# Four engines issue in the order of the source, and the source emits the steps of all parts by a plan of engine times

## The chip, the cores and the metric

The kernel runs on one core of one Trainium2 chip. The metric is the device time of one execution in microseconds. The core has five engines that matter here: TensorE (PE: matrix products and transposes; PEld is its loading of weights), VectorE (DVE), ScalarE (ACT), GpSimd (POOL, which here issues the transfers that scatter and gather rows by an index) and SyncE (SP, which issues all other transfers). Each engine executes its own list of instructions and waits on semaphores for the others.

## The reference

Two macaron layers on 2048 tokens (2 sequences of 1024) of 256 numbers, all in 32-bit floats:

```
x = x + 0.5 * L0_ffn(layernorm(x))      # 8 experts of width 176, top 2, and a shared expert of width 352
x = x + L0_attn(layernorm(x))           # RWKV: time mix, then channel mix
x = x + 0.5 * L0_ffn(layernorm(x))
x = x + 0.5 * L1_ffn(layernorm(x))      # 32 experts of width 96, top 6, and a shared expert of width 192
x = x + L1_attn(layernorm(x))           # linear attention with rotary embedding: one sum over each sequence
x = x + 0.5 * L1_ffn(layernorm(x))

# an ffn: scores -> the top K experts of each token and their weights ->
g = silu(x @ w_gate[e]) * (x @ w_up[e]);  routed = sum over the K experts of weight * (g @ w_down[e])
out = routed + (silu(x @ sw_gate) * (x @ sw_up)) @ sw_down
```

## The kernel before, in words

x stays in SBUF as 16 tiles of 128 tokens. Each of the four ffn parts (`sparse_moe`) sorts the tokens by expert through DRAM:

- **Routing** (`ready`, in halves of 8 tiles): `prep` normalizes four tiles (L108 to L114 on DVE, a square root on ACT), transposes them on PE (L122), copies the result on ACT (L299), multiplies by the router (L303), and finds the top experts on DVE (L140 to L180). After two preps `plan` counts tokens by expert with two products (L336, L343) and computes a slot in DRAM for every pair of token and expert (to L392). After the second half `owners` finds which expert owns each block of 128 slots (`who`, L425 and L426).
- **Scatter** (L399): one transfer on POOL for each tile and each of its K experts writes the rows to their slots in `xs`. That is 16 transfers a half in L0 and 48 in L1.
- **Shared expert** (`shared`, L452 gates, L468 turn, L494 output, L501 the addition to x) and the pairs' weights (`weights`, DVE).
- **Blocks**: 39 blocks of 128 slots in L0, 127 in L1. A block is fetched (L509, SP), transposed (L518), copied (L522, ACT), multiplied with its expert's gate and up weights, whose number PE reads from `who` (L531), gated (L442 ACT, L443 DVE), turned (L468, L475), multiplied with the down weights (L546), copied (L554, DVE) and stored (L555, SP). The stages of five neighbouring blocks alternate. A fetch waits for all scatters.
- **Combine**: a transfer on POOL gathers the rows of one tile and one expert (L565) into one of eight buffers, and four calls later DVE adds them to x with their weight (L576). The first half's gathers wait for the blocks that can hold its rows (23 in L0, 79 in L1) and go beside the remaining blocks. The second half's wait for the last block.

Between the first and the second L0 ffn stands RWKV: eight jobs (time mix and channel mix on four groups of four tiles), `run` calling the preparation of the next job inside the one before it. Its weights are loaded by `load_rwkv` (L644 to L655), which also computes five small vectors 1 - v on DVE (L652). `fill_slots` writes zeros to all slots of `xs` ahead of time. The attention (`attend`, once for each sequence) normalizes and transposes eight tiles, then multiplies each with the input weights (L833), rotates, sums, transposes the queries (L883) and at last multiplies with a scaled output matrix (L908).

The order of instructions on each engine is chosen by the Tile framework's scheduler, which takes the source's order as priority and a cost model's times for when something can start. In the source the parts stand one after another. The first L0 ffn reads

```
m["dispatch"](0)      # ready and scatter of the first half
m["dispatch"](1)
load_rwkv(weights)
m["shared"](0)
...
finish(m["blocks"](2))
```

and a few pairs alternate by fixed rates: the first combine beside the last blocks (2 calls a block in L0, 1 in L1), the first L1 routing beside the last L0 blocks, the first attention beside the second combine of the first L1 ffn.

## Time and profile before

17 executions took 1743.61 to 1756.22 us, with a median of 1749.77. The profiled execution took 1746.8 us, and its span from the first to the last instruction is 1745.0 us, at a mean granted clock of 0.82.

| stage | us from the start | length |
|---|---|---|
| first L0 ffn: routing, scatter, shared | 0 to 130 | 130 |
| its blocks | 130 to 243 | 113 |
| its second combine | 243 to 269 | 26 |
| RWKV | 269 to 480 | 211 |
| second L0 ffn: routing, scatter, shared | 480 to 597 | 117 |
| its blocks | 597 to 722 | 125 |
| its second combine; first L1 ffn: routing, scatter, shared | 722 to 920 | 198 |
| its blocks | 920 to 1157 | 237 |
| first attention and second combine | 1157 to 1209 | 52 |
| second L1 ffn: routing, scatter, shared; second attention | 1209 to 1438 | 229 |
| its blocks | 1438 to 1675 | 237 |
| its second combine | 1675 to 1745 | 70 |

The stages are read from the first and last start of their lines (L518 and L554 for blocks, L692 for RWKV, L908 for the end of an attention). POOL was busy for 523.6 us, 497 of them with the 512 indirect transfers, 0.97 us each, of which two neighbours start 1.26 us apart.

### The profile page before, as it was taken

Reading aid. Unit: us, or ns where it says so; the run is one execution under the profiler, and the core shown is the slowest. Engines: PE = TensorE matmul, PEld = TensorE weight load, DVE = VectorE, ACT = ScalarE, POOL = GpSimd, SP = SyncE. Lnnn points to the kernel's source line nnn. Section 1 sums busy time; section 2 is a strip of 40 time slices with the busy share of each in tenths; the row PEclk is TensorE's granted clock in tenths of the full one; section 3 lists DMA queues with packets and bytes.
Section 4 is the critical chain, followed back from the end, with each engine's and each line's share of the span. In section 5 each row is a group of like instructions: output and inputs, shape, how many; then the busy total and the mean of one; then the engine's idle time right before and its main releaser. Section 6 shows DMA issues by size and latency. Waiting matters only on the chain.

```text
span 1745.0 us, 21541 instructions
## 1 busy us (share of the span) xinstructions
PE 1205.0 (69%) x5462; PEld 899.5 (52%) x5462; DVE 759.5 (44%) x2588; ACT 580.4 (33%) x1565; POOL 523.6 (30%) x559
## 2 busy tenths in 40 slices
PE   6599856899957997511549994795837409994830
PEld 5377533566745775411328983663514309873630
DVE  5322348666153234332414443657826604443433
ACT  4123225776341333300105541441402105541310
POOL 1500321111133003274630016225570550016246
PEclk8699987999977999855669996897768759996875
DMA  9503329200081133541215664542220125665543
GB/s 278 184 16 104 121 85 305 89 1 0 0 204 64 31 103 118 147 137 63 91 66 158 188 182 136 154 125 70 69 103 10 67 90 171 184 183 157 172 123 106
DMA packets 182911, 203.06 MB, mean 116 GB/s; under 512 B 40044, under 2 KB 165772, under 8 KB 182796
## 3 DMA queue, kind: packets, MB, share of 16 engines
q1 hardware_dynamic: 158220, 134.55, 25.9%
q0 software_dynamic: 24576, 67.14, 12.3%
q8 instruction: 52, 0.85, 0.2%
q14 instruction: 63, 0.52, 0.1%
HBM read 100.68 MB, written 100.93 MB: 116 GB/s over the span
## 4 chain that ended last, share of the span: by engine, by line
PE 42%; issue 24%; another core or an unknown queue 6%; DVE 5%; DMA 3%; POOL 3%; ACT 2%; POOLq 0%; SPq 0%; DVEq 0%; ACTq 0%
PE pg_L_b L531 12%; PE py_L_b L546 8%; PE px_L L518 4%; PE pkv_cm L704 3%; POOL yk_L L565 3%; PE pkk_cm L692 3%; PE pg_L L452 3%; DMA yk_L<-ys_L,idx_L 2%; PE ph_L_b L468 2%; PE py_L L494 2%; DVE x L576 1%; PE pk_tm L692 1%; PE pcr_cm L704 1%; DMA ys_L<-yb_L 1%
## 5 line engine op out<-in xcount | busy, mean ns | idle before, releaser
L565 POOL DMA_INDIRECT yk_L<-ys_L,idx_L x256 | 248.1, 969 | 733.3 <-DMA ys_L<-yb_L 481.1
L399 POOL DMA_INDIRECT xs_L<-xn_L,idx_L x256 | 248.9, 972 | 287.6 <-DVE who_L L426 77.8
L531 PE MATMUL pg_L_b<-L1gu,xbT_L 128*128 x1016 | 223.8, 346 | 12.8 <-issue 8.7
L443 DVE TENSOR_TENSOR h_L_b<-g_L_b,pg_L_b 128x96 f32<-128x96 f32 (+1 forms) x332 | 90.4, 273 | 325.2 <-ACT g_L_b L442 299.1
L522 ACT COPY xbT_L<-px_L 128x256 f32<-128x256 f32 x332 | 123.4, 373 | 243.6 <-PE px_L L518 208.8
L531 PEld LDWEIGHTS pg_L_b<-L1gu,xbT_L 128*128 128x128 f32 x1016 | 170.7, 202 | 18.5 <-issue 11.4
L576 DVE SCALAR_TENSOR_TENSOR x<-yk_L,wk_L,x 128x256 f32<-128x256 f32 x256 | 120.0, 480 | 124.1 <-DMA yk_L<-ys_L,idx_L 108.8
L546 PE MATMUL py_L_b<-L1down,hT_L_b 96*128 x508 | 162.3, 402 | 12.7 <-ACT g_L_b L442 4.5
L518 PE MATMUL px_L<-ident,xb_L 128*128 128x128 f32 x664 | 133.0, 283 | 52.1 <-issue 52.1
L554 DVE COPY yb_L<-py_L_b 128x256 f32<-128x256 f32 x332 | 140.6, 423 | 63.1 <-PE py_L_b L546 33.2
L468 PE MATMUL ph_L_b<-ident,h_L_b 128*96 128x128 f32 (+1 forms) x410 | 103.3, 283 | 66.7 <-issue 38.7
L442 ACT ACTIVATE g_L_b<-pg_L_b 128x96 f32<-128x96 f32 (+1 forms) x332 | 88.4, 266 | 181.3 <-PE pg_L_b L531 118.3
L518 PEld LDWEIGHTS px_L<-ident,xb_L 128*128 128x128 f32 x664 | 97.5, 148 | 90.0 <-issue 57.3
L531 PE MATMUL pg_L_b<-L0gu,xbT_L 128*128 x312 | 108.4, 470 | 1.1 <-issue 0.6
L475 ACT COPY hT_L_b<-ph_L_b 96x128 f32<-96x128 f32 (+1 forms) x332 | 93.1, 280 | 38.7 <-PE ph_L_b L468 19.0
L468 PEld LDWEIGHTS ph_L_b<-ident,h_L_b 128*96 128x96 f32 (+1 forms) x410 | 51.6, 128 | 97.3 <-issue 56.3
L546 PEld LDWEIGHTS py_L_b<-L1down,hT_L_b 96*128 96x128 f32 x508 | 81.2, 201 | 24.9 <-ACT hT_L_b L475 6.2
L452 PE MATMUL pg_L<-L0sgu,xTs_L 128*128 128x352 f32 x256 | 90.8, 493 | 0.0
L442 ACT ACTIVATE g_L<-pg_L 128x176 f32<-128x176 f32 (+1 forms) x96 | 29.8, 323 | 166.1 <-PE pg_L L452 93.5
L546 PE MATMUL py_L_b<-L0down,hT_L_b 88*128 x312 | 82.8, 388 | 1.1 <-ACT hT_L_b L475 1.1
L122 PE MATMUL pt_L<-ident,xn_L 128*128 128x128 f32 x128 | 25.9, 349 | 67.4 <-DVE mv_L L109 31.4
L501 DVE SCALAR_TENSOR_TENSOR x<-py_L,x 128x256 f32<-128x256 f32 x64 | 27.0, 422 | 97.2 <-PE py_L L494 47.0
(216 smaller groups left out, 1849.7 us busy)
## 6 DMA issues: line engine op xcount, KB each, us to landing
xb_L<-xs_L SPq DMA_DIRECT2D x332, 128.0 KB
ys_L<-yb_L SPq DMA_DIRECT2D x332, 128.0 KB
xs_L<-zero SPq DMA_DIRECT2D x1, 16256.0 KB
xs_L<-zero SPq DMA_DIRECT2D x1, 4992.0 KB
xs_L<-xn_L,idx_L POOLq DMA_INDIRECT x256
yk_L<-ys_L,idx_L POOLq DMA_INDIRECT x256
L1gu<-in_L_gate SPq DMA_DIRECT2D x8, 384.0 KB
L1gu<-in_L_up SPq DMA_DIRECT2D x8, 384.0 KB
```

The source lines that it names most:

```text
L399: d = nc.gpsimd.indirect_dma_start(out=xs, out_offset=bass.IndirectOffsetOnAxis(ap=idx[:, t, k : k + 1], axis=0), in_=xn[h][:, i, :], in_o ...
L442: nc.scalar.activation(g, pg[:, 0:width], AF.Silu)
L452: nc.tensor.matmul(pg, xT[half][:, c, i * P : (i + 1) * P], w["sgu"][:, c, u, :, :].rearrange("p z w -> p (z w)"), start=(c == 0), stop=(c ...
L468: nc.tensor.transpose(pt[0:m, k * P : (k + 1) * P], h[:, r : r + m], ident)
L475: nc.scalar.copy(hT[0:m, lo:hi, :].rearrange("p k t -> p (k t)"), pt[0:m, lo * P : hi * P])
L518: nc.tensor.transpose(px[:, c * P : (c + 1) * P], xb[:, c * P : (c + 1) * P], ident)
L522: nc.scalar.copy(xbT.rearrange("p c t -> p (c t)"), px[:, 0 : DC * P])
L531: nc.tensor.matmul(pg, xbT[:, c, :], w["gu"][:, c, bass.ds(e, 1), :, :].rearrange("p e z h -> p (e z h)"), start=(c == 0), stop=(c == DC - 1),
L546: nc.tensor.matmul(py, hT[0:HP, k, :], w["down"][:, bass.ds(e, 1), k, :].rearrange("p e d -> p (e d)"), start=(k == 0), stop=(k == C - 1),)
L554: nc.vector.tensor_copy(yb, py)
L565: d = nc.gpsimd.indirect_dma_start(out=yk, out_offset=None, in_=ys[0 : n * P, :], in_offset=bass.IndirectOffsetOnAxis(ap=idx[:, t, k : k + ...
L576: added = nc.vector.scalar_tensor_tensor(x[t], gathered.pop((t, k)), wk[:, t, k : k + 1], x[t], ALU.mult, ALU.add)
```

## The change

Two parts of the program, the first L0 ffn and everything from the second L0 ffn to the end, are put into `manual_schedule` for PE, DVE, ACT and SP: these engines issue in the order in which the source emits instructions. RWKV and POOL are left to the scheduler. Every part becomes a generator that yields, after each step, an engine and the time that the step takes on it. `side_by_side` keeps a clock for each part and for each engine, and always emits the next step of the part whose clock is earliest; `after` lets a part begin when named other parts have been emitted. The plan knows these times only; nothing of it is measured while the program runs.

```diff
+    free = dict.fromkeys(("PE", "DVE", "POOL"), 0.0)
+    def side_by_side(*parts):
...
+            n = min(able, key=lambda n: (clocks[n], n))
+            if clocks[n] > clock["now"]:
+                yield "until", clocks[n]
+            step = next(parts[n], None)
...
+                engine, us = step
+                clocks[n] = max(clock["now"], free.get(engine, 0.0)) + us
+                if engine:
+                    free[engine] = clocks[n]
...
             normalize(x[ts], xb, BT, sub)
+            yield "DVE", 3.4
+            yield "", 1.0
             for c in range(DC):
                 nc.scalar.copy(xT[h][:, c, o * P : o * P + TB], transposed(xb, c, sub))
+            yield "PE", 1.0
+            yield "", 1.0
...
             route(w, lg, sub, taken[:, ts, :], comb[:, ts, :])
+            yield "PE", 1.3
+            yield "DVE", 3.0 if K == 2 else 4.0
...
+                    yield "POOL", 1.28
...
                     nc.vector.scalar_tensor_tensor(x[t], py, 0.5, x[t], ALU.mult, ALU.add)
+                yield "PE", 0.0033 * (SH * DC + D)
...
-        def combine(h, lag=4):
+        def combine(h, lag=4, adding=True, late=None):
             pairs = [(t, k) for t in range(HT * h, HT * h + HT) for k in range(K)]
-            for n in range(len(pairs) + lag):
+            for n in range(len(pairs) + (lag if adding else 0)):
                 if n < len(pairs):
-                    gather(*pairs[n])
-                if n >= lag:
+                    gather(*pairs[n], back if n < 8 or late is None else late)
+                if adding and n >= lag:
                     add_back(*pairs[n - lag])
-                yield
+                yield "POOL" if n < len(pairs) else "", 1.3
+            done[f"combine{h}"] = True
...
-            side = combine(0)
-            for q in range(NBLK + 4):
-                if q < NBLK:
-                    fetch(q)
+            for q in range(-lead, NBLK + 4):
+                if 0 <= q + lead < NBLK:
+                    fetch(q + lead)
...
+                if q - 4 == first - 1:
+                    done["first"] = True
+                yield "PE", 0.00169 * DC * 2 * H + 0.00169 * C * D + 0.1 * (DC + C)
...
+        return [
+            after([(d, "ready0"), (d, "ready1")], m["scatter"](1)),
+            after([(d, "ready0"), *alone], shared_of(0), m["weights"](0)),
+            after(
+                [(d, "ready1"), (d, "shared0")],
+                shared_of(1),
+                m["weights"](1),
+                after([(d, "scatter0"), (d, "scatter1")], m["blocks"]()),
+            ),
+        ]
...
-            m["dispatch"](0)
-            m["dispatch"](1)
-            load_rwkv(weights)
-            m["shared"](0)
...
+            with tc.manual_schedule(engines=ORDERED):
+                load_rwkv(weights)
+                play(
+                    after([], m["ready"](0), m["ready"](1)),
+                    after([(d, "ready0")], m["scatter"](0)),
+                    *mixture(m),
+                    after([(d, "first")], m["combine"](0)),
+                )
+        for _ in m["combine"](1, adding=False, late=weights):
+            pass
...
+                for t in range(HT, NT):
+                    for k in range(w0["K"]):
+                        m["add_back"](t, k)
+                        tc.add_manual_dep(
+                            m["latest"]["add"], rw["latest"].name, NOSYNC, reason="rows come late"
+                        )
...
+    with tc.manual_schedule(engines=ORDERED):
+        play(
+            after([], m0["ready"](0), m0["ready"](1)),
+            after([(d0, "ready0")], m0["scatter"](0)),
+            after([(d0, "blocks")], then(last_weights)),
+            *mixture(m0),
+            after([(d0, "first")], m0["combine"](0)),
+            after([(d0, "combine0"), (d0, "blocks")], m0["combine"](1)),
+            after([(d0, "combine0")], m1["ready"](0)),
+            after([(d1, "ready0"), (d0, "combine1")], m1["scatter"](0)),
+            after([(d1, "ready0"), (d0, "combine1")], m1["ready"](1)),
+            *mixture(m1, [(d0, "blocks")]),
+            after([(d1, "first")], m1["combine"](0)),
+            after([(d1, "combine0"), (d1, "blocks")], m1["combine"](1)),
+            after([(d1, "combine0"), (d1, "blocks")], attend(0, moe_pool)),
+            after([(at, "done0")], m2["ready"](0)),
+            after([(d2, "ready0"), (d1, "combine1")], m2["scatter"](0)),
+            after([(d2, "ready0"), (d1, "combine1")], attend(1, moe_pool), m2["ready"](1)),
+            *mixture(m2),
+            after([(d2, "first")], m2["combine"](0)),
+            after([(d2, "combine0"), (d2, "blocks")], m2["combine"](1)),
+        )
```

Smaller edits go with it. The two preps of a half alternate. In the first L0 ffn the second half's 16 gathers are issued without their additions, eight of them into eight new buffers, and the additions are emitted after the first mixing of the first RWKV job. The fetch of a block is emitted two steps earlier. The attention's tile steps are shifted: the products of tile t stand before the sums and queries of tile t-1 (a step planned at 4.6 us of PE), and the two additions to x move into the sums. Scratch tiles of `weights` and `plan` move from the three "yb" buffers to the four "xb" buffers, and the tiles of an ffn are allocated when its half begins.

## The prediction

> **What bounds the kernel now.** I read the page first, then the table by stage, then the tensor engine's timeline inside the poorest stage, then the DMA queue's own timeline. The page says that no engine is full on average:
>
> ```profile
> span 1745.0 us, 21541 instructions
> ...
> PE 1205.0 (69%) x5462; PEld 899.5 (52%) x5462; DVE 759.5 (44%) x2588; ACT 580.4 (33%) x1565; POOL 523.6 (30%) x559
> ...
> PE   6599856899957997511549994795837409994830
> ...
> POOL 1500321111133003274630016225570550016246
> ...
> L565 POOL DMA_INDIRECT yk_L<-ys_L,idx_L x256 | 248.1, 969 | 733.3 <-DMA ys_L<-yb_L 481.1
> L399 POOL DMA_INDIRECT xs_L<-xn_L,idx_L x256 | 248.9, 972 | 287.6 <-DVE who_L L426 77.8
> ```
>
> The reader sees PE near full in the blocks and the RWKV part, and almost empty where POOL's digits are high: where rows are scattered (L399) and gathered (L565). The table by stage (columns: stretch, length, busy time of PE, weight loads, DVE, ACT, POOL, then granted clock, DMA share, GB/s) puts lengths to it:
>
> ```profile
> 0.00:36.00 36.00, 23.32 (x84) 17.52 (x85) 22.37 (x137) 15.05 (x24) 1.74 (x14) 0.88 0.95 283
> 36.00:130.00 94.00, 71.20 (x301) 53.89 (x300) 27.49 (x146) 23.56 (x67) 31.22 (x33) 0.81 0.38 113
> 504.00:597.00 93.00, 68.21 (x295) 51.32 (x294) 26.95 (x142) 23.05 (x67) 30.74 (x32) 0.83 0.23 70
> 722.00:920.00 198.00, 63.58 (x209) 43.35 (x207) 52.34 (x213) 17.24 (x41) 108.54 (x112) 0.59 0.34 106
> 920.00:1039.00 119.00, 118.60 (x750) 106.41 (x749) 55.59 (x165) 64.54 (x251) 0.00 (x0) 1.00 0.60 182
> 1039.00:1157.00 118.00, 82.25 (x401) 66.88 (x401) 58.72 (x180) 40.02 (x138) 46.11 (x48) 0.78 0.50 149
> 1249.00:1438.00 189.00, 81.77 (x305) 52.11 (x304) 78.34 (x296) 30.50 (x75) 94.29 (x96) 0.71 0.20 70
> 1560.00:1675.00 115.00, 78.57 (x391) 64.90 (x389) 49.47 (x138) 33.45 (x129) 46.29 (x48) 0.78 0.55 162
> 1675.00:1745.00 70.00, 0.00 (x0) 0.00 (x0) 23.24 (x48) 0.00 (x0) 45.35 (x48) 0.51 0.38 107
> ```
>
> The two L1 dispatch stages (198 and 189 us) hold 64 and 82 us of PE work. L1 blocks run at 1.42 us each until the gathers begin (the yb copies at 958.5 to 1015.3 are 40 blocks in 56.8 us) and at 4.1 us beside them (20 from 1038.0 to 1119.6). Inside the 198 us stage, PE's timeline shows why (start, length, work, idle before it):
>
> ```profile
> 781.48 1.11 PE L122 MATMUL pt_L<-ident,xn_L 128*128 128x128 f32 x4 [19.56 <-issue]
> 793.69 0.63 PE L303 MATMUL lg_L<-L1router,xTs_L 128*128 128x32 f32 x2 [11.09 <-issue]
> 804.89 3.19 PE L303 MATMUL lg_L<-L1router,xTs_L 128*128 128x32 f32 x14 [10.57 <-issue]
> 820.61 1.19 PE L336 MATMUL rank_L<-taken_L,before 128*128 128x256 f32 x2 [12.53 <-DVE taken_L L168]
> ```
>
> Nothing that these steps wait for is late; the fourteen products at 804.89 are read by ACT only at 818.31. PE itself crawls, and it does so beside requests that POOL issues back to back (one per 1.26 us from 751.1 to 810.5). I call this the crawl. It begins some 10 to 13 us after such a train begins: shared tiles start every 2.4 us from 841.0 to 845.8 in the train from 833, and the adds that follow come at 860.0, 871.3 and 882.5.
>
> **The change part by part.** No arithmetic operation is added or removed; order and buffers move. The working is against the profiled execution: 1745.0 us of span, 1746.8 us in all, 3 us under the median of 1749.8.
>
> *The five small DVE operations at the top (a loss).* The loads of the RWKV weights and the operations 1-mk and so on (L652) now stand first in the ordered part, ahead of the first normalization on DVE. Their loads stand behind the x, L0 and zero transfers on SP:
>
> ```profile
> 52.88 0.49 SPq L648 DMA_DIRECT2D v_cm_mk<-in_cm_mk  x1
> 53.41 0.47 SPq L648 DMA_DIRECT2D v_cm_mr<-in_cm_mr  x1
> ```
>
> SP's order up to here does not change. The issue is paced by earlier landings, and the scatters of 36 to 57, which shared the DMA engines, will not have begun; with 2.2 us to land (x: issued at 0.74, read at 2.93) I put the fifth operation at 53. The before kernel executed them at 76.0 to 80.3, where nobody waited. Everything on DVE queues behind them: the first normalization starts at 53 instead of 2.9, and PE, ACT and POOL wait for it. The first half's routing then takes the 22 us that it took with data at hand (480 to 502) instead of 33, and ends at 75 instead of 36.
>
> *Shared experts beside the second half's routing (L0, twice).* Before, only gates were pulled forward; the shared turns waited for the routing's last product (who_L, at 66 and 533). Now they alternate. PE work after the first routing: 16 tiles by 4.0 us (adds at 107.2, 111.2, 115.2) are 64, routing of the second half 8, the crawl beside two 20 us trains 5 (12 gates by 2.4 and 16 outputs by 1.7 are 56 us, 538 to 597 took 59), and 8 for PE reaching a routing step too early and for ACT's table loads (1.28 us each; ACT is busy 23.6 of 94 us, so most are covered). Sum 85. First dispatch: blocks at 75 + 85 = 160 against 130, **-30** (+9 if the loads did not gate it). Second: 503 + 85 = 588 against 597, **+8**. Ends for the pair: -45 and +22.
>
> *L0's second combine moved into RWKV's first job.* Blocks ended at 243 and the first RWKV product came at 269; the 16 adds stood between. They go behind the first mixing; 16 by 0.48 are 7.7 us of DVE, while the first jobs wait on DVE anyway (reciprocals of 3.3 us). Gathers use fresh buffers. **+5**; ends -8 and +13.
>
> *L1's first dispatch.* Let the L0 blocks end at 0 (722 before). Gathers 9 to 29, first scatter 29 to 90 (48 by 1.27). The shared half is 19 us of PE (8 by 2.4): from 8 to 20 at full pace, the rest in the crawl, at a quarter (14 us of routing products stood in 63 us, 755 to 818), to 48. The second routing, now behind it on PE, has 14 us of PE work: 8 to 10 in the crawl by 90, the rest and 12 of DVE chain to 105. Second scatter 105 to 166, blocks at 168 against 198: **+30**. Ends: 0 (the crawl deepens), and +45 (POOL alone: 29 + 61 + 61 + 2).
>
> The Trainium skill, "SBUF — State Buffer", section "Who interferes with whom", says that PE and ACT never wait on anyone and that DMA does not contend with a compute engine. By that rule the overlapped work runs at full pace and the three L1 terms here and below give 45 + 45 + 45 instead of 54 in all. The rows above contradict it, so the sum does not use it.
>
> *L1 blocks beside the first combine, twice.* 237 us now: 79 blocks by 1.42, 4 for the store, then the slow stretch. Calls come once per planned block as before, eight gather buffers allow POOL ten us of lead, and then each gather waits for an add. With PE at 0.4 pace while POOL issues (20 blocks, 28 us of work, in 71 us), a block lasts 1.42 + 0.6 by 1.25 = 2.17; 48 of them are 104: 112 + 4 + 104 + 5 = 225. **+12** each. Four calls are 5.2 us of lag; store, gather and landing take about 8 (gather at 1039.34, its add at 1042.60, 3.3 us, behind a store of 4 to 5), so DVE stalls once for 3 us, included. On SP, now in source order, a block's fetch stands three steps (4.3 us) ahead of its use with one store between; a fetch lands in 2.0 us (1429.19), so I cost that at nothing. Ends for each: -10 and +45.
>
> *Attention and last dispatch.* attend(0), 52 us, now in two shifted steps: **+3**. attend(1) shares PE with a shared half (19 us) that had been done during the routing (adds 1244.7 to 1259.2). From the routing's end at T: 64 us of PE work, 13 before the crawl, 14 in it to T+61, 37 behind: T+98 against T+93 (1249 to 1342). **-5**; ends -25 and +20. Scatter and last combine stay: the 70 us at the end have no PE to be put beside.
>
> Sum: -30 + 8 + 5 + 30 + 24 + 3 - 5 = +35, so 1746.8 - 35 = 1712 in a profiled run, 1715 against the median; I say 1713.
>
> **The rivals.**
> *The small operations do not gate the start.* Either DVE takes them late, or they land early. Then the first dispatch gains 9 instead of losing 30: 1674. For: x takes the same queue and lands by 15.5. Against: the v loads are issued behind 12 MB. Chance 0.14.
> *The adds pace POOL so that there is no train and no crawl beside the blocks.* The combine beside attend(0) (1160 to 1236, POOL held eleven times by an add) shows no crawl. Both block stages gain 47 instead of 12: 1713 - 70 = 1643. Chance 0.10.
> *The crawl eats it.* More PE work lies beside trains; the L1 dispatch and both block stages gain nothing: 1713 + 54 = 1767, slower. Chance 0.14.
> *The plan runs ahead of the engines.* Slower: PE reaches routing steps whose inputs are late and holds the tiles behind them. There are 16 preparations with three such places each (transposes, logits, rank), 48. The plan gives a normalization 4.4 us; the first one took 2.93 to 9.0, 6.1. At 1.7 us each that is 82: 1795. It decides from 35/48 = 0.7 us each. Against: the plan gives an L0 shared tile 3.17 us and it takes 4.0, so PE comes later than planned. Chance 0.20.
>
> **How the numbers follow.** Main 0.42, own range 1670 to 1745; rivals as above. Faster by over 0.2% (3.5 us, about what a measurement here can tell): 0.40 + 0.14 + 0.10 = 0.64. Slower: 0.34 less what falls within, 0.32. Same 0.04. The range 1640 to 1798 leaves out half of the 1643 case, half of the 1795 case and little else, under 0.2.
>
> **What would show it.** The first L108 on DVE near 53, with L652 before it; the first block (L518) at 160, and shared outputs (L494) before the second routing's end. From the last L0 block to the first L1 block 168 us. yb copies beside gathers 2.2 us apart. The last scatter behind attend(1) as now. A first L108 at 3 refutes the loss; copies 1.4 apart refute the crawl there; PE idle with a releaser on DVE or ACT before L122 and L303, 48 times, is the last rival.

## The result: 5.4% slower on the chip of the prediction, 3.2% slower on another kind of chip

The changed kernel took 1841.45 us (median of 8, 1838.32 to 1846.09) against 1748.37 us (median of 47): a ratio of 1.0535, 95% interval 1.0518 to 1.0552. Predicted were 1713 us and a gain. The profiled execution took 1851.15 us, 10 us above the median, and the lengths of stages below are its own. The page of the profile after, whose lines answer to those shown of before:

```profile
span 1849.1 us, 21526 instructions
...
PE 1257.9 (68%) x5462; PEld 921.5 (50%) x5462; DVE 801.2 (43%) x2588; ACT 558.1 (30%) x1551; POOL 521.0 (28%) x559
...
PE   0588986799978898633528997954635545998830
...
POOL 0231033111022103174360005455360071003546
...
L627 POOL DMA_INDIRECT yk_L<-ys_L,idx_L x256 | 247.1, 965 | 730.2 <-DMA ys_L<-yb_L 547.2
L455 POOL DMA_INDIRECT xs_L<-xn_L,idx_L x256 | 247.8, 968 | 379.9 <-DVE idx_L L446 128.1
```

The transfers cost POOL what they did, PE and DVE execute as many instructions as before (5462 and 2588), and PE's first digit has gone from 6 to 0. The two groups of low digits (3352, slices 18 to 21, and 54635545, slices 27 to 34) are the L1 dispatches, the second with both attentions, where PE was meant to become fuller. The table by stage after (columns as before: stretch, length, PE, weight loads, DVE, ACT, POOL, granted clock, DMA share, GB/s):

```profile
0.00:50.00 50.00, 0.00 (x0) 0.00 (x0) 0.53 (x3) 0.00 (x0) 2.06 (x15) 1.00 0.92 253
50.00:177.00 127.00, 93.19 (x384) 70.59 (x385) 54.07 (x272) 34.36 (x88) 31.03 (x32) 0.91 0.18 63
516.00:641.00 125.00, 96.89 (x388) 72.20 (x386) 52.04 (x260) 33.09 (x87) 31.58 (x33) 0.81 0.36 92
772.00:983.00 211.00, 79.78 (x220) 51.71 (x220) 60.40 (x228) 17.80 (x43) 108.43 (x112) 0.60 0.32 99
1114.00:1205.00 91.00, 76.52 (x398) 59.91 (x396) 48.33 (x139) 34.41 (x133) 45.74 (x48) 0.92 0.67 196
1205.00:1318.00 113.00, 62.78 (x194) 41.24 (x194) 85.44 (x286) 15.75 (x48) 47.37 (x48) 0.67 0.20 58
1318.00:1553.00 235.00, 109.57 (x340) 71.20 (x340) 90.81 (x310) 38.76 (x90) 92.73 (x96) 0.67 0.16 54
```

For 50 us POOL and DVE show 2.6 us of work and the others none. The first L1 dispatch, 198 before, lasts 211. The last one, 189 before, lasts 235; the first shared half has come into it (340 records of PE, before 305).

One more thing has to be known to read what follows. The kernel before took 1748 us on the chip of the prediction and 1760 on another, but 1589 to 1591 on five more that runs were given. (Each of these was met in one set of runs, so a lasting property of a chip is not told from its state at that time.) So each experiment is compared with the kernel before on its own chip, and I call the first kind *chips with the crawl*: it is the crawl, as the prediction named it, that the others lack. The same cuts on both kinds (us, from the starts of the same lines; "routed" is the first half's slots being known):

| stage | before, after: with the crawl | difference | before, after: without | difference |
|---|---|---|---|---|
| start to first L0 block | 130, 177 | -47 | 111, 158 | -47 |
| L0 blocks | 113, 111 | +2 | 113, 103 | +10 |
| RWKV, up to routed | 260, 253 | +7 | 260, 254 | +6 |
| up to first block of the second L0 ffn | 94, 100 | -6 | 74, 80 | -6 |
| its blocks | 123, 131 | -8 | 125, 117 | +8 |
| up to first L1 block | 199, 211 | -12 | 155, 151 | +4 |
| L1 blocks | 238, 222 | +16 | 230, 209 | +21 |
| first attention, second combine, up to routed | 92, 113 | -21 | 87, 105 | -18 |
| up to first block of the second L1 ffn | 189, 235 | -46 | 138, 174 | -36 |
| its blocks | 236, 225 | +11 | 226, 208 | +18 |
| rest | 71, 71 | 0 | 71, 71 | 0 |

There are three losses: the start (47 on either kind), the stretch around the two attentions (54 without the crawl), and what the crawl adds (before lost 155 us to it, after 219, so 64 more). The gains in the blocks are there, and larger where nothing crawls.

### The profile page after: what moved, and what is told of

It is laid out like the page before. It is cut to its first block, busy times and chain, and to the rows that moved or that the text cites. A ratio compares the mean times of both kernels' runs of the same rounds, so it can differ in the third digit from the quotient of the medians.

```text
span 1849.1 us, 21526 instructions
## 1 busy us (share of the span) xinstructions
PE 1257.9 (68%) x5462; PEld 921.5 (50%) x5462; DVE 801.2 (43%) x2588; ACT 558.1 (30%) x1551; POOL 521.0 (28%) x559
## 4 chain that ended last, share of the span: by engine, by line
PE 44%; DVE 14%; another core or an unknown queue 11%; issue 7%; DMA 4%; ACT 3%; POOL 1%; POOLq 0%; DVEq 0%; ACTq 0%; SPq 0%
PE pg_L_b L593 12%; PE py_L_b L608 7%; PE px_L L580 4%; PE pg_L L513 3%; PE pkv_cm L761 3%; PE pkk_cm L749 3%; PE py_L L555 2%; DMA xb_L<-xs_L 2%; PE ph_L_b L529 2%; DVE x L638 2%; PE lg_L L354 2%; DMA yk_L<-ys_L,idx_L 1%; PE po_at L761 1%; PE ph_L L529 1%
## 5 line engine op out<-in xcount | busy, mean ns | idle before, releaser
L593 PEld LDWEIGHTS pg_L_b<-L1gu,xbT_L 128*128 128x128 f32 x1016 | 164.5, 196 | 37.4 <-issue 23.4
L608 PE MATMUL py_L_b<-L1down,hT_L_b 96*128 x508 | 155.6, 388 | 0.3 <-ACT hT_L_b L536 0.2
L638 DVE SCALAR_TENSOR_TENSOR x<-yk_L,wk_L,x 128x256 f32<-128x256 f32 x256 | 121.1, 480 | 59.1 <-DMA yk_L<-ys_L,idx_L 51.7
L529 PE MATMUL ph_L<-ident,h_L 128*128 128x128 f32 (+1 forms) x160 | 35.5, 322 | 147.1 <-DVE h_L L504 78.2
L580 PEld LDWEIGHTS px_L<-ident,xb_L 128*128 128x128 f32 x664 | 93.5, 145 | 68.0 <-DMA xb_L<-xs_L 15.5
L529 PE MATMUL ph_L_b<-ident,h_L_b 128*96 128x128 f32 (+1 forms) x410 | 102.0, 280 | 17.5 <-DVE h_L_b L504 10.3
L529 PEld LDWEIGHTS ph_L<-ident,h_L 128*128 128x128 f32 (+1 forms) x160 | 21.3, 151 | 175.3 <-DVE h_L L504 86.3
L504 DVE TENSOR_TENSOR h_L<-g_L,pg_L 128x176 f32<-128x176 f32 (+1 forms) x96 | 31.6, 342 | 164.9 <-issue 82.9
```

The costliest lines, as they stand in the source:

```text
L504: nc.vector.tensor_tensor(dst, g, pg[:, width : 2 * width], ALU.mult)
L529: nc.tensor.transpose(pt[0:m, k * P : (k + 1) * P], h[:, r : r + m], ident)
L580: nc.tensor.transpose(px[:, c * P : (c + 1) * P], xb[:, c * P : (c + 1) * P], ident)
L593: nc.tensor.matmul(pg, xbT[:, c, :], w["gu"][:, c, bass.ds(e, 1), :, :].rearrange("p e z h -> p (e z h)"), start=(c == 0), stop=(c == DC - 1),
L608: nc.tensor.matmul(py, hT[0:HP, k, :], w["down"][:, bass.ds(e, 1), k, :].rearrange("p e d -> p (e d)"), start=(k == 0), stop=(k == C - 1),)
L638: added = nc.vector.scalar_tensor_tensor(x[t], gathered.pop((t, k)), wk[:, t, k : k + 1], x[t], ALU.mult, ALU.add)
```

## The experiments

**The five small operations.** In the changed kernel they gate the start, as DVE's timeline says (start, length, work, idle before it and what ended it):

```profile
50.41 0.17 DVE L708 TENSOR_SCALAR u_tm_mk<-v_tm_mk 128x2 f32<-128x2 f32 x1 [48.55 <-DMA v_tm_mk<-in_tm_mk]
...
52.40 0.17 DVE L708 TENSOR_SCALAR u_cm_mr<-v_cm_mr 128x2 f32<-128x2 f32 x1 [0.47 <-DMA v_cm_mr<-in_cm_mr]
52.48 0.42 DVE L109 BATCH_NORM_STATS2 st_L<-x 128x6 f32<-128x256 f32 x1
```

```diff
-            if "_m" in v:
-                u = pool.tile([P, DC], F32, name=f"u_{v}")
-                nc.vector.tensor_scalar(u, t, -1.0, 1.0, ALU.mult, ALU.add)
-                rw[f"1-{v}"] = u
...
+    def complements(pool):
+        for v in ("tm_mk", "tm_mv", "tm_mr", "cm_mk", "cm_mr"):
...
+                    after([(d, "blocks")], then(lambda: complements(weights))),
```

> The changed kernel with one edit: the five small DVE operations 1 - v of the RWKV weights are emitted behind the last block of the first L0 ffn instead of ahead of its first normalization; the loads stay where they are. Theory (DVE issues in order, so they hold the whole start until their data lands at 50 us): the first normalization starts near 3 us, the first block near 133 instead of 177, and the time falls by about 44 us, 1841 to 1797. Rival (the start is held by the x rows or by the tensor engine's own order): the first block stays within 10 us of 177, the time within 10 us of 1841.

On a chip with the crawl: 1803.96 us, ratio 1.0251 (1.0233 to 1.0268) instead of 1.0535: 2.8%, or 50 us of this chip's 1760. The first block came at 130 instead of 177. DVE's timeline of this run:

```profile
2.74 0.43 DVE L109 BATCH_NORM_STATS2 st_L<-x 128x6 f32<-128x256 f32 x1 [2.74 <-DMA x<-in_x]
```

The theory stands. Half of the whole loss is five operations of 0.17 us in front of an ordered queue.

**Shared work out of the way.** Two runs on the same chip move the shared halves of the L1 ffns.

```diff
-            *mixture(m1, [(d0, "blocks")]),
+            *mixture(m1, [(d0, "blocks"), (d1, "ready1")]),                                      # m1_hold
-            after([(d2, "ready0"), (d1, "combine1")], attend(1, moe_pool), m2["ready"](1)),
+            after([(d2, "shared0"), (d1, "combine1")], attend(1, moe_pool), m2["ready"](1)),     # m2_first
```

> The changed kernel with one edit: in the first L1 ffn the shared experts of the first half wait in the plan until the second half's routing is emitted. Theory (shared steps that crawl beside POOL's transfers stand ahead of the combine's additions and of the second routing on DVE and PE): the second routing ends 111 us behind the last L0 block as in the kernel before, instead of 131; both shared halves then lie beside the second scatter and end some 10 us behind it; the stage takes about 191 instead of 211, and the time falls by about 20 us to 1821. Rival (the routing crawls as well, whoever stands ahead of it): the routing ends within 5 us of 131, the stage takes 211 or more, and the time stays at 1841 or rises.

1847.68 us, ratio 1.0489 (1.0465 to 1.0513). Half of its theory came true: the routing came back to 112 us behind the last block. The stage did not move: 772 to 984, 212 us, as the rival had it. All 16 shared tiles now lay beside the second scatter, which began at 885, and their additions ran from 893 to 978. The 0.5% that the ratio is lower I cannot place in the trace.

> The changed kernel with one edit: in the second L1 ffn the shared experts of the first half are emitted whole, ahead of the second attention, instead of in turns with it. Theory (in turns both last through the crawl; ahead of it the shared half is done at full pace in the first 20 us of the scatter): the second attention ends about 95 us behind the first routing instead of 125, and the time falls by 25 to 32 us to about 1812. Rival (the attention crawls by itself, the shared half costs its own 19 us wherever it stands): the time stays within 6 us of 1841.

1855.86 us, ratio 1.0554 (1.0530 to 1.0578): this theory falls, and the rival stands. The attention did its products at 3.7 us a tile instead of 10.5 in turns, but it did them behind the scatter, which ended at 1377, and its first product came 81 us behind the routing instead of 14: five shared tiles were done by 1339, the other three took until 1383. The stage took 243 us instead of 235. In these two runs the order of the work beside a train changed little; whatever stood there crawled.

**The crawl by itself.** I measured it in a program of its own, one phase after another:

```
for phase, works in enumerate(PHASES):
    tc.strict_bb_all_engine_barrier()
    for kind, args in works:        # scatter, gather, direct, busy on one side; shared, dense, chain on the other
        ...
```

> A program of its own, which leaves the whole computation out and returns x: nine phases with a barrier of all engines ahead of each. The work is 32 tiles of the L1 shared expert (as in the kernel: two products into 384 columns, two transposes, two products into 256), beside, in order: nothing; 48 scatters; 48 gathers by index; 48 plain reads of the same size issued by SP; 60 additions on POOL; 48 scatters with a long memset on POOL behind every eighth. Then 32 times four products into 512 columns beside 48 scatters; then a chain of 60 transposes, each waiting for a copy of the one before, alone, and beside 48 scatters. Theory (requests that POOL makes slow TensorE, to 2.7 us for a weight load and product, from some 20 us into an unbroken train): 77 us for 32 tiles alone, beside plain reads and beside POOL's additions; 100 to 110 us beside scatters and beside gathers, with products 2.4 to 2.8 us apart from 20 us on to the train's end; less than 90 with the pauses. Rival 1 (it is the traffic of the rows): the plain reads slow it as much. Rival 2 (it is not the requests but what the kernel's steps wait for): 77 to 80 us in every one of the first six phases.

It ran once, on a chip with the crawl. From the first addition of the 32 tiles to the last it took 120 us beside scatters and 122 beside gathers, and 71 in the other four of the first six phases: 50 us more, where the theory had 23 to 33. The table by windows, those with requests from POOL cut to the time in which it made them: nothing; 48 scatters; 48 gathers; plain reads; POOL's additions; scatters with pauses:

```profile
66.00:138.00 72.00, 71.67 (x304) 50.52 (x302) 24.10 (x62) 19.32 (x61) 0.00 (x0) 1.00 0.00 1
138.00:200.00 62.00, 26.56 (x84) 16.25 (x84) 5.51 (x15) 5.00 (x15) 46.38 (x48) 0.69 0.28 100
265.00:325.00 60.00, 22.76 (x72) 13.83 (x71) 4.61 (x12) 4.35 (x13) 45.39 (x48) 0.70 0.35 103
392.00:469.00 77.00, 76.42 (x321) 53.53 (x322) 24.94 (x64) 20.64 (x64) 0.03 (x1) 1.00 0.28 82
469.00:536.00 67.00, 67.00 (x281) 46.87 (x282) 21.33 (x55) 18.35 (x57) 62.37 (x60) 1.00 0.00 1
546.00:617.00 71.00, 71.00 (x298) 49.54 (x298) 22.41 (x58) 18.92 (x61) 57.22 (x54) 1.00 0.25 89
```

(In the trace a 32-bit product is two records, a transpose one.) About 300 records of PE in 70 us, but 84 and 72 in 60 us beside requests that POOL makes without a break. Plain reads and additions on POOL cost nothing, so neither these bytes nor a busy POOL is the cause. (The reads' 6.3 MB moved in the first 27 us of their phase, at some 250 GB/s; beside scatters and gathers the crawl had begun 13 to 16 us into theirs, at 100 GB/s.) With 1.8 us of pause behind every eighth request no tile took more than 3.9 us. The chain shows the onset, 27 us into its train:

```profile
836.99 0.47 PE L152 MATMUL pc<-ident,gc 128*128 128x128 f32 x1 [0.36 <-issue]
837.82 0.48 PE L152 MATMUL pc<-ident,gc 128*128 128x128 f32 x1 [0.36 <-issue]
840.53 0.48 PE L152 MATMUL pc<-ident,gc 128*128 128x128 f32 x1 [2.24 <-issue]
843.33 0.48 PE L152 MATMUL pc<-ident,gc 128*128 128x128 f32 x1 [2.32 <-issue]
```

A step goes from 0.83 to 2.8 us. The granted clock (third number from the end) is not the cause; it was 0.50 in the 25 us ahead of the onset and in the 34 us behind it, with 30 and 13 records:

```profile
811.00:836.00 25.00, 14.28 (x30) 5.49 (x30) 0.00 (x0) 8.03 (x31) 18.90 (x21) 0.50 0.28 100
837.00:871.00 34.00, 6.17 (x13) 2.36 (x13) 0.00 (x0) 3.19 (x12) 25.91 (x27) 0.50 0.29 105
```

Products of 512 columns beside 48 scatters, at a granted clock of 1.0 until then, fell to 8 records in 22.4 us, 2.8 each, from 34 us on. So it is some 2 us more for each weight load with its product, with 128 columns as with 512. The kernel after shows the same; one shared tile of its first L1 dispatch (the engine's idle time and its releaser in brackets):

```profile
823.78 0.33 ACT L503 ACTIVATE g_L<-pg_L 128x192 f32<-128x192 f32 x1 [19.87 <-remote]
824.56 0.66 PE L529 MATMUL ph_L<-ident,h_L 128*96 128x128 f32 x2 [15.96 <-issue]
829.44 0.37 ACT L536 COPY hT_L<-ph_L 96x256 f32<-96x256 f32 x1 [5.33 <-remote]
829.86 2.08 PE L555 MATMUL py_L<-L1sdown,hT_L 96*128 96x256 f32 x4 [4.64 <-issue]
840.59 0.42 DVE L562 SCALAR_TENSOR_TENSOR x<-py_L,x 128x256 f32<-128x256 f32 x1 [16.09 <-remote]
851.79 0.33 ACT L503 ACTIVATE g_L<-pg_L 128x192 f32<-128x192 f32 x1 [21.98 <-remote]
```

Two transposes until 829.44 (2.4 us each), the four records of the output until 840.59 (2.7), the four of the gates until 851.79 (2.8): 28 us for a tile that takes 2.4. Ends of products are modelled in the trace, so the waits of ACT and DVE show it better than PE's own lengths.

**The same on chips without it.** The next four runs, and all that followed, met chips where the kernel before took 1589 to 1591.

> The program of the first probe (it leaves the computation out and returns x) with other trains. 32 shared tiles beside: nothing; 48 scatters with a pause on POOL behind every eighth of 0.5 us; behind every fourth of 0.3 us; behind each of 0.1 us; behind every sixteenth of 1.8 us; 48 unbroken scatters of 64 rows instead of 128; 48 gathers with 1.8 us behind every eighth. Then the chain of 60 transposes beside 48 unbroken scatters and beside 48 with 1.8 us behind every eighth. Theory (requests pile up somewhere and a pause lets the pile drain, so the share of paused time counts): 1.8 us behind every eighth request keeps every stretch at 71 to 80 us, for gathers and for the chain (50 us) too; 0.5 us behind eight, a quarter of that share, leaves a crawl (over 90 us); 1.8 behind sixteen leaves a crawl in the second half of every sixteen; 64 rows a request make a smaller pile and less crawl. Rival (an unbroken run of requests alone counts, not the time paused): any of the pauses, the shortest too, ends the crawl, and 64 rows crawl as 128 do.

> The second probe again (it leaves the computation out and returns x), beside a kernel before that shows which kind of chip it is. Theory (on a chip with the crawl, where the kernel before takes about 1750, the time in which POOL makes no request counts): 1.8 us of pause behind every eighth request keeps gathers and the chain at their own pace (71 and 50 us), 0.5 us behind eight and 0.3 us behind four shorten the crawl without ending it, 1.8 behind sixteen leaves one in each sixteen, 64 rows a request crawl less. Rival: any pause ends it. On a chip where the kernel before takes about 1590 nothing crawls in any phase: 71 us each.

Both ran where nothing crawls: additions 2.4 us apart in all seven phases, and the chain 0.83 us a step beside unbroken scatters. They show that the crawl is a matter of the chip (or of its state when it was met), and nothing of which pause would do. The chain kept its 0.83 us at a granted clock of 0.50 here too. What differs between the chips, and where in the machine the 2 us are spent, stays open.

> The changed kernel once more, on the chip that the next three run on. The chips that runs were given differ: on two the kernel before took 1748 and 1760 us, on a third 1591, where the chain of transposes beside unbroken scatters kept its 0.83 us a step. Theory (the third chip has no crawl, everything else alike): where the kernel before takes about 1590, this takes 1635 to 1650 and its L1 dispatch stages are near 150 and 180 us instead of 211 and 268; where it takes about 1750, this takes 1840 to 1855 as before. Rival (the third chip is faster in general): all stages are shorter by the same tenth.

> The kernel before, for its trace on this chip. Theory: where it takes about 1590, its blocks without POOL keep their 1.42 us, its RWKV part keeps its 211 us, and the 160 us are gone from the stages in which POOL issues: 198 and 189 in the L1 dispatches, 118 and 115 in the blocks beside the first combine. Rival: all stages are shorter by a tenth.

1636.93 us against 1588.94 us: ratio 1.0324 (1.0281 to 1.0368). The stage table above is from these two. RWKV keeps its 260 us and the blocks without POOL theirs (119 with the crawl, 122 without), so the chips are alike but for the stages in which POOL issues; the rival falls. But of the 118 and 115 us of the blocks beside the first combine 108 and 104 are left, so the crawl was only 10 and 11 of them. What slows these blocks is DVE's order, as the lines of the kernel before show over its 48 gathers (960 to 1022), and those of the changed kernel over the same (991 to 1063), both without the crawl:

```profile
L576 DVE SCALAR_TENSOR_TENSOR x<-yk_L,wk_L,x 128x256 f32<-128x256 f32 x46 | 21.2, 481 | 32.6 <-DMA yk_L<-ys_L,idx_L 32.5
L468 PE MATMUL ph_L_b<-ident,h_L_b 128*96 128x128 f32 x16 | 6.6, 410 | 21.1 <-DVE h_L_b L443 21.1
```

```profile
L638 DVE SCALAR_TENSOR_TENSOR x<-yk_L,wk_L,x 128x256 f32<-128x256 f32 x41 | 19.5, 477 | 4.0 <-DMA yk_L<-ys_L,idx_L 4.0
L529 PE MATMUL ph_L_b<-ident,h_L_b 128*96 128x128 f32 x39 | 10.8, 278 | 0.3 <-DVE h_L_b L504 0.3
```

Before, some three additions stand in DVE's order for each block (46 beside 16), DVE waits 32.5 us for their rows, and PE waits 21 us for the blocks' gates behind them: 3.75 us a block. After, one addition stands for each block (41 beside 39), and DVE waits 4 us: 1.85 us a block.

**Pauses in the kernel.**

```diff
+        if calls["n"] % 8 == 0:
+            for _ in range(5):          # 4 in both_pause, and there not behind second combines
+                z = nc.gpsimd.tensor_tensor(quiet, quiet, quiet, ALU.add)
```

> The changed kernel with one edit: behind every eighth scatter or gather POOL makes five additions on a small tile of its own, some 2 us, and POOL's requests keep the order of the source. Theory (the crawl is what the overlapped work loses, and a pause every 10 us ends it, as in the probe): the trains become 20% longer (48 requests 71 us instead of 61), and no product beside them lasts longer than its normal time; the L1 dispatch goes from 211 to about 175, the second from 268 to about 225, the two stretches of L1 blocks from 222 and 225 to about 200, the last combine from 70 to 80; the time falls by 90 to 120 us, to about 1735. Rival (POOL's requests set those stages, the crawl lies beside them): four to six trains of 61 us become 10 us longer each, and the time rises by 40 to 60 us to about 1890.

> The kernel before with the same edit and nothing else. Theory: its L1 dispatch stages crawl too (35 to 60 us of each), and its blocks beside the first combine; the L1 blocks go from 237 to about 210 each, the dispatch stages gain 10 to 20 each against 20 lost on longer trains, the last combine loses 10: the time falls by 30 to 70 us, to about 1700. Rival (POOL sets those stages): the time rises by 40 to 60 us.

On a chip without the crawl: 1703.01 us, ratio 1.0711 (1.0681 to 1.0740), and 1689.58 us, 1.0637 (1.0604 to 1.0670). The pauses (320 additions, 154 us of POOL) cost the kernel before 99 us, more than its rival said, and the changed kernel 66. The edit also holds POOL's requests to the source's order, and no run separates the two. The shorter ones:

> The kernel of the run named both, with four small additions on POOL (some 1.9 us) behind every eighth scatter and every eighth gather of a first half. Theory (a pause every 10 us ends the crawl): on a chip with the crawl each stage falls to what it is on a chip without, plus 12 us for each scatter of 48 rows' tiles that stands in the chain: the L1 dispatch to about 175, the second from 235 behind its first routing to about 200, the L1 blocks to 205 to 210, 100 to 135 us in all, faster than the kernel before by 3 to 6%. On a chip without the crawl it is slower than the run named both by 50 to 70 us. Rival (the crawl does not come from unbroken trains in the kernel): slower by 50 to 70 us on any chip.

> The run named m2_early with 1.9 us of small additions on POOL behind every eighth scatter and every eighth gather of a first half. Theory: on a chip with the crawl it loses 100 us or more to it without the pauses, and gains them against 35 us for the pauses (measured without the crawl: 1618 against 1584): 0.93 to 0.97 of the kernel before. On a chip without the crawl: 30 to 40 us slower than m2_early. Rival (unbroken trains are not what makes it in the kernel): 30 to 60 us slower than m2_early on any chip.

> The kernel of the run named both_pause again, on whichever chip it gets. Theory: where the kernel before takes about 1750 (slow products beside POOL's unbroken requests), the pauses take the slow products away and the ratio to the kernel before is 0.92 to 0.97, against 1.025 for the same kernel without the pauses and with the attention planned as in the change. Where it takes about 1590: 1.018, as measured. Rival (unbroken trains are not what makes the slow products in the kernel): 1.03 to 1.06 where the kernel before takes about 1750.

1617.57, 1614.08 and 1618.82 us (ratios 1.0185, 1.0157, 1.0187); the first two are 34 and 31 us above the same kernels without pauses on the same chips. None met a chip with the crawl. That pauses pay there is shown by the probe alone, not in the kernel.

**The order around the attentions.**

```diff
-            yield "PE", 4.6
+            yield "PE", 4.6 if s else 2.1        # at_step; "both" is u_late and this together
```

> The changed kernel with one edit: a tile step of the first attention is planned at 2.1 us of TensorE instead of 4.6, so that the plan puts one or two of the combine's additions between two tiles instead of three or four. Theory (the additions in DVE's order hold the attention's own steps, and each waits for a gather): the first attention goes from 80 to about 55 us, the first routing behind it takes the rest of the additions and ends 100 us behind the last block instead of 113, and the time falls by 10 to 20 us. Rival (POOL's 48 gathers, 61 us, and the attention's own DVE work set the end of the pair): the routing ends within 4 us of 113, and the time does not change.

> The changed kernel with two edits: the five small DVE operations behind the last block of the first L0 ffn, and the first attention's tile steps planned at 2.1 us of TensorE. Theory: the first gives 45 to 50 us on any chip, the second 10 to 20 where the additions pace the attention: 1.5 to 2% above the kernel before on a chip with the crawl, within 1% of it on one without. Rival: the second edit gives nothing (the sum of POOL's 48 gathers stays), and the ratio is that of the first edit alone, 1.025 on a chip with the crawl.

> The kernel of the run named both. Where the kernel before takes about 1750: 1.025 by the first edit's measured 50 us alone, 1.02 if the second gives what it gave without the crawl. Where it takes about 1590: 0.997 as measured.

The step plan alone: 1631.41 us, 1.0272 (1.0243 to 1.0300), 0.5% under the changed kernel, with intervals that overlap; the stage went from 105 to 98 and the next from 174 to 178. The lengths in its expectation are those of a chip with the crawl. With the small operations moved as well: 1583.75 us, 0.9972 (0.9951 to 0.9993), and on another chip 1580.52, 0.9955 (0.9936 to 0.9974). So without the crawl the moved operations decide the sign, and the rest of the change comes to next to nothing: its gains in the blocks go into the losses around the attentions. (No run moved the operations alone on such a chip.)

> The run named both, and in the second L1 ffn the first shared half is emitted as soon as its rows are turned, beside the routing's DVE steps, and the second attention behind it instead of in turns with it. Theory (without the crawl the changed kernel still loses 36 us between the first routing's end and the first block, 174 against 138, because the shared half had been done before the routing ended in the kernel before and is now in turns with the attention): the stretch falls from 178 to about 150, the time by 20 to 30 us, to about 1560, 0.98 of the kernel before; with the crawl by 5 to 20 us. Rival (the attention's own steps in source order are slow, whatever stands between them): the stretch stays within 8 us of 178.

1583.43 us, 0.9960 (0.9945 to 0.9975): no gain, the stretch still 178 us. The shared half was done 16 us into it, but the attention's normalization stood behind it in DVE's order, its first product came at 1148 instead of 1141, and its sum was complete at 1189 instead of 1190. The rival stands, so the last run took the written order away:

```diff
-            after([(d1, "combine0"), (d1, "blocks")], attend(0, moe_pool)),
-            after([(at, "done0")], m2["ready"](0)),
...
+    rest = m1["combine"](1)
+    beside(attend(0, moe_pool), rest, 1.6)
+    beside(m2["ready"](0), rest, 1.2)
+    finish(rest)
+    finish(m2["scatter"](0), m2["shared"](0), attend(1, moe_pool), m2["ready"](1), ...)
...
+    with tc.manual_schedule(engines=ORDERED):
+        play(m2["blocks"](), ...)
```

> The run named both, and one stretch taken out of the written order: from the last L1 block of the first L1 ffn to the first block of the second (its second combine, both attentions, both routings, scatters and shared halves) the scheduler orders the engines again, from the kernel before's source; the L0 part, the first L1 ffn and all blocks keep the written order. Theory (in those two stages the written order costs: the second attention starts its products 31 us behind the first routing instead of 11 and takes 4.6 us a tile instead of 3.3): where the kernel before takes about 1590, the two stages fall from 276 to about 225 us and the time from 1582 to about 1532, 0.963 of the kernel before; where it takes about 1750, from about 1.022 to 0.985. Rival (the stages are set by POOL's transfers and the length of the routing, and the scheduler's order only starts the scatter later): the two stages stay within 10 us of 276 and the ratio at 0.996, or 1.022 where the kernel before takes 1750.

1527.81 us, ratio 0.9608 (0.9586 to 0.9630), with 0.963 expected: 53 us under "both", and faster than both kernels on a chip without the crawl. The two stages, first of "both" (second run), then of this one:

```profile
1022.00:1119.00 97.00, 60.08 (x194) 39.30 (x194) 79.80 (x274) 16.39 (x50) 44.71 (x46) 0.72 0.21 63
1119.00:1296.00 177.00, 94.50 (x340) 64.24 (x340) 97.19 (x324) 31.40 (x83) 97.64 (x99) 0.72 0.21 75
```

```profile
1026.00:1110.00 84.00, 60.67 (x219) 38.57 (x220) 71.59 (x279) 25.26 (x62) 49.14 (x48) 0.82 0.27 78
1110.00:1249.00 139.00, 76.66 (x309) 52.23 (x307) 78.03 (x292) 30.34 (x75) 94.46 (x96) 0.76 0.27 93
```

274 become 223. In the first stage the scheduler normalized half of the attention's rows (four of eight tiles, at 991) beside the last blocks, so that its first product came with the last block instead of 9 us behind it. In the second (from routed): first attention product at 10 us instead of 22, its sum complete 30 us later instead of 49, second routing 34 instead of 42, then 65 and 64 to the first block. The attention's shifted steps are still in this source, so the shift by itself is not what costs. It was not run on a chip with the crawl.

## Why the prediction was wrong

Its sum was +35; measured, in the stages of the two profiled executions, -104.

- **The small operations: -30 predicted, -47 measured.** The mechanism and its instant were right: L109 came at 52.5, predicted 53. Moving them gave 50 us where the prediction had 39 between gated and not gated. The first routing behind them took 27 us instead of 22, and the second routing with the shared experts 97 instead of 85; without the crawl these took 80 (79 to 158, the predicted block at 160). So the mis-sized term is "the crawl beside two 20 us trains 5": 97 against 80 makes it 17.
- **Second L0 dispatch: +8 predicted, -6.** The same term failed in the sum of 85 from the first routing on: the stretch took 100 us with the crawl (541 to 641) and 80 without, 20 us for the 5. Without it, 80 us stand against 74, of which PE worked 72 (the predicted 64 and 8) and 66; PE had been busy there all along, and there was nothing to win.
- **Combine in RWKV: +5 predicted, +7.** Right.
- **First L1 dispatch: +30 predicted, -12 or -13.** The mis-sized term is "the rest in the crawl, at a quarter". A shared tile took 28 us in it, a twelfth of its pace. I had read a quarter from stretches that also held idle time and full pace, and sized it by work; it goes by the number of products, 2.4 to 2.8 us a record. The first shared half lasted until 880, the combine's additions stood behind it on DVE (L638 at 813, 841, 864 to 870), and the second routing behind those, 132 us behind the last block instead of 112. Holding the shared half back returned the 20 and lost them again behind the routing. Without the crawl it is +4, 155 to 151, POOL's own 153 that the prediction gave as an end. The gain of 30 was to come out of the crawl of the kernel before (199 us against 155 without it), and none of the orders run on a chip with the crawl took it away: the stage stayed at 210 to 212 in the four kernels with the written order (after, u_late, m1_hold, m2_first).
- **L1 blocks beside the combine: +12 each predicted, +16 and +11.** 222 and 225 us for a predicted 225, but by luck. The price is of the wrong wait: "PE at 0.4 pace while POOL issues" put the slow blocks of the kernel before down to the crawl, and without the crawl they are nearly as slow (3.75 us each), by additions that wait for rows in DVE's order. One addition a block is what the written order gains by, 21 and 18 us without the crawl. Two misses of size cancel besides. The last 48 blocks took 1.95 us each in the first of the two stages (94 us) and not 2.17. Ahead of them the written order took 120 us for 79 blocks, between first and last copy, instead of 111 (without the crawl 118 and 111): PE stood idle for 7 us before the blocks' transposes, 2 of them ended by a fetch, and before for none. The prediction put the fetches and this stretch at no loss.
- **First attention: +3 predicted, -21 up to routed.** The step that failed is "now in two shifted steps". I counted the steps and not what the scheduler had put elsewhere: the normalization (before at 1112 to 1122, beside blocks that ended at 1157; after at 1205 to 1213) and the rate of additions (3 to 4 of them between two tiles, DVE 85 us of 113 instead of 67 of 92). Planning fewer of them returned 7 us of the stage without the crawl (105 to 98), the scheduler's order another 13 (97 to 84).
- **Second attention: -5 predicted, -46.** I costed the shared half's 19 us of PE and nothing for the written order. Without the crawl the stage still loses 36: from routed to the first product 14 us (11 before), to the complete sum 54 (28), second routing 42 (34), then 64 (65). In turns, the crawl makes 101 of the 54. Free_mid shows that the written order as a whole costs this; how much each reordering costs is only read from the traces, and on a chip with the crawl it was not run.
- **Blocks of the second L0 ffn: 0 predicted, -8 with the crawl, +8 without.**

Of the rivals, "the crawl eats it" (1767, chance 0.14) named the right cause for the L1 dispatch, but had the blocks gain nothing where they gained 16 and 11, and its floor of no gain was no floor: the overlapped work lost where it stood ahead of the next routing. 40 of the 104 us are lost without any crawl. "The small operations do not gate" and the paced combine are refuted by L109 and the 222 and 225 us. "The plan runs ahead" looked at the wrong waits. Without the crawl PE's idle time over the whole program before the routing's products (L354, L390, L393, L484) is 57 us against 51 before; what grew is the wait of the shared turns (L529), 29 us instead of 1, for an h that stands behind the routing's steps in DVE's order.

The prediction set a rule of the Trainium skill, "SBUF — State Buffer", section "Who interferes with whom", against its rows: that PE and ACT never wait on anyone. With the crawl the measurement differs and decides (84 records in 62 us beside a train against 304 in 72 alone). Without it, the same tiles ran at 2.4 us beside such a train, as the page says.

## What to carry over

Before operations are put in front of a queue that issues in order, look at when their data lands: five operations of 0.17 us cost 50 us here. When a scheduler's order is replaced by a written one, list what it had pulled forward into other stages (a normalization, gates, additions); each of those is a term of the sum. Before a slow stretch is put down to one cause, look at which wait ends last in it. And before work is moved beside another engine's stage, measure one piece of it there, by instructions and not by busy time, and on more than one chip.

## What the runs showed that I had not expected

The same program took 1748 to 1760 us on some chips and 1589 to 1591 on five others, 10% apart, with nearly equal times where POOL issues nothing (119 and 122 us for the L1 blocks ahead of the gathers). Where it is slow, each weight load with its product takes some 2 us more, beginning some 10 to 34 us into an unbroken series of indirect requests, until it ends or pauses (1.8 us in every 12 was enough in the probe), for scatters as for gathers. ACT's and DVE's instructions kept their lengths in it (0.33 and 0.42 us in the tile above). On a chip of the other kind an unbroken series of 48 cost PE nothing.
